# Graph attention with a pre-norm: the next group's norm, softmax and attention moved within the group, and a two-level product scheme for the second projection

## The chip, the cores and the metric

The kernel runs on one core of one Trainium2 chip. A core has five engines with their own instruction queues: TensorE multiplies matrices (the profile shows its weight loads apart, as PEld), VectorE (DVE), ScalarE (ACT) and GpSimd (POOL) work on tiles element by element, and SyncE (SP) issues transfers. The metric is the device time of one execution, in microseconds, and a kernel's time is the median of its runs.

## The reference

The input x has 128 graphs of 64 nodes with 512 features, in float32, and all graphs share one adjacency matrix of 64 x 64. Everything is computed in float32. Per graph:

```
h = relu(layernorm(x))
for each of 4 heads:  Wh = h @ W_head            # 512 x 512
    e = leaky_relu(f1[:, None] + f2[None, :])    # f = Wh . a, two scalars per node
    A = softmax(where(adj > 0, e, -1e9))         # 64 x 64
    head = elu(A @ Wh)
out = elu(one more such attention of concat(heads), with W_out: 2048 x 512)
y = relu(out @ w1 + b1) @ w2 + b2 + out
result = x + layernorm(y) * gamma + beta
```

## The kernel before

**Tiles and groups.** Rows of x are taken 128 at a time (two graphs make a tile), four tiles make a group (`G = 4`), and there are 16 groups. The loop over groups (`for g in range(NG)`, line 817) has two stages: a head stage, with the first projection of the four heads (`project1`), and a second stage with the second projection (`project2`). The other work is slipped between their steps.

**Products.** A 512 x 512 by 512 x 512 product is done on four quadrants of 256 with seven products in place of eight (Strassen's scheme in Winograd's form). `unit` (line 260) runs the seven products 1 to 7 in a given order and collects their sums in three PSUM banks, `after` moves sums out by VectorE and ScalarE, and `post` stores the results. One product has four float32 matmuls for each matrix, and each of those appears in the trace as two matmul instructions with 256 moving columns. The sums of weight quadrants are made once by `weight_sums` (line 199) on GpSimd and kept in device memory (`TC`); `piece` (line 227) loads one 256 KB piece of weights into a ring of 11 buffers, on SP's queue, ahead of its use. In `project2` the four heads are four matrices that add up in the same bank, so that it has 28 pieces; its operands are the four quadrant blocks `H1`, and GpSimd turns them in place into the sums that later products need (line 615).

**The group's attention.** Attention comes ahead of the head projection: A is applied to the normalized rows, and then the head's weights. `norm1` (line 352) normalizes one tile: statistics on VectorE, a power and a product on GpSimd, the activation on ScalarE. `transpose_h` and `project_f` give the scores, `attn_weights` runs the softmax on VectorE and ScalarE, `transpose_weights` turns the weights, `attend1` (line 510) multiplies, its results go through the six PSUM banks shared with the products (tag `mm`) and are copied half by ScalarE and half by VectorE. `z_sums` makes the operand sums of a head on GpSimd. `stage_a` (line 480) collects norm, scores and turns of a group.

**Around the second projection.** The list of steps of `project2(g)` is interleaved by `run` and `mix` with attention of group g+1 (`attend1`, then `z_sums` for its first head), norm and softmax of group g+2, and the feed-forward of group g-1 (`feed_forward`, line 690: transposes, two units of seven products, and `finish`, which normalizes a tile and stores it). The second attention of group g-1 (`stage_e`) stands in the head stage of g. In group 0 the head stage has norm and scores of group 1 and the weight sums of W_out.

**Order.** The order in which a helper is called gives priorities; a planner that works with estimated costs and with the buffers of each tag orders the instructions of every engine from these, and `tc.high_priority(AHEAD)` raises the evacuations. Each engine and SP's queue then work strictly in that order, so that an instruction that waits holds all behind it.

The lines that set the order of the second stage for an inner group are

```
run(project2(g), first + mix(
    ff[:7] + early + ff[7:12] + fin[:1] + ff[12:13] + fin[1:2] + ff[13:],
    scores + [nothing] * 8,
) + mix(fin[2:], [nothing] + turns + [nothing] * 2))
```

Of the kernel before, what the change touches and what calls it, by code (L numbers as in the profile page):

```python
# [18 lines left out]
AHEAD = 150  # L19


@with_exitstack
def gat_preln_kernel(
# [47 lines left out]
    ring = ctx.enter_context(tc.tile_pool(name="ring", bufs=11))  # L71
# [20 lines left out]
    def load(t, name="x"):  # L92

        tl = wk.tile([P, F], FP, tag="x", name=f"{name}{t}", bufs=4)
        nc.sync.dma_start(out=tl, in_=xf[ts(t, P), :])
        return tl
# [47 lines left out]
    MT, TC = {}, {}  # L144
    DIRECT = {}

    def fetch(m):
        MT[m] = big.tile([P, KC, O], FP, tag=homes[m], name=f"pw{m}")
        queue = nc.scalar if m < H else nc.gpsimd
        queue.dma_start(out=MT[m], in_=mats[m].rearrange("(k p) o -> p k o", p=P))  # L150
# [13 lines left out]
    def turn_a():  # L164

        rows = H * 2 * KC
        pt = aux([P, rows], "pah")
        nc.tensor.transpose(pt, ah, ident[0:rows, 0:rows])
        aT = wk.tile([P, H, 2, KC], FP, tag="s1", name="aT")
        nc.scalar.copy(aT.rearrange("p h c o -> p (h c o)"), pt)  # L170
        return aT

    def fold_dve(m, ab):

        for k in range(KC):
            for c in range(2):
                junk = wk.tile([P, O], FP, tag="t", name=f"jk{c}_{m}_{k}")
# [21 lines left out]
    def weight_sums(m, after=None):  # L199
# [20 lines left out]
        TC[m] = [dram.tile([P, 2, 2, Q], FP, name=f"tc{m}_{i}") for i in range(2)]  # L220
# [19 lines left out]


    late = []
# [17 lines left out]
    def unit(name, product, post, order):  # L260
# [5 lines left out]
        def after(p):  # L266
            if p in (1, 5, 6):
                nm = {1: "s1", 5: "s5", 6: "t"}[p]
                sb[nm] = wk.tile([P, 2, T], FP, tag=nm, name=f"{nm}_{name}")
# [30 lines left out]
    def product_t(m, blocks):  # L300

        def product(p):
            def fn(bk, start):
                w, a = piece(m, p), blocks(p)
                for o in range(2):
                    for k in range(2):
                        nc.tensor.matmul(  # L307
# [6 lines left out]
    def product_n(ms, blocks):  # L314

        def product(p):
            def part(i):
                def fn(bk, start):
                    w, a = piece(ms[i], p), blocks(p, i)
                    for k in range(2):  # L320
                        for j in range(2):
                            nc.tensor.matmul(  # L322
# [17 lines left out]
    def norm_stats(src, tag, t):  # L340

        st = sm.tile([P, 6], FP, tag=tag + "st", name=f"{tag}st{t}")
        nc.vector.bn_stats(st, src)
        mv = sm.tile([P, 2], FP, tag=tag + "mv", name=f"{tag}mv{t}")
        nc.vector.bn_aggr(mv, st)
        ve = sm.tile([P, 1], FP, tag=tag + "ve", name=f"{tag}ve{t}")
        nc.vector.tensor_scalar(ve, mv[:, 1:2], EPS, None, ALU.add)  # L347
        rstd = sm.tile([P, 1], FP, tag=tag + "rs", name=f"{tag}rs{t}")
        nc.gpsimd.tensor_tensor(rstd, ve, mhalf, ALU.pow)
        return mv[:, 0:1], rstd  # L350

    def norm1(t):
        if t not in X:
            X[t] = load(t)
        mean, rstd = norm_stats(X[t], "n1", t)
        nb = sm.tile([P, 1], FP, tag="n1nb", name=f"n1nb{t}")
        nc.gpsimd.tensor_scalar(nb, mean, rstd, -1.0, ALU.mult, ALU.mult)
        HN[t] = big.tile([P, F], FP, tag="hn", name=f"hn{t}", bufs=G)
        nc.scalar.activation(HN[t], X.pop(t), AF.Relu, bias=nb, scale=rstd)
        if t % G >= 2:  # L360
            HNS[t] = big.tile([P, T], FP, tag="hns", name=f"hns{t}", bufs=2)
            nc.gpsimd.tensor_tensor(HNS[t], HN[t][:, 0:T], HN[t][:, T:2 * T], ALU.add)
# [12 lines left out]
    def project_f(g):  # L375
# [15 lines left out]
        eng = nc.vector if g == 0 else nc.gpsimd  # L391
        eng.tensor_tensor(
# [65 lines left out]
    A1, E1, LAST = {}, {}, {}  # L458
# [4 lines left out]
    def transpose_weights(p):  # L463
        A = A1.pop(p)
        for j in range(2):
# [7 lines left out]
            AT[t] = big.tile([P, NB, H, N], FP, tag="at", name=f"at{t}", bufs=G)  # L473
# [6 lines left out]
    def stage_a(g):  # L480


        if g >= NG:
            return [], [], []
        p, r = 2 * g, 2 * g + 1

        def norms(p):
            norm1(2 * p)
            norm1(2 * p + 1)
            if p >= 2:  # L490
                prefetch(2 * p + 2)
                prefetch(2 * p + 3)

        def transposes(p):
# [3 lines left out]
        return (  # L498
            [lambda: norms(p), lambda: norms(r)],
            [  # L500
                lambda: transposes(p), lambda: transposes(r), nothing, lambda: project_f(g), nothing,
                lambda: (scores1(g), attn_weights(p)), nothing, lambda: attn_weights(r),
            ],
            [nothing, lambda: transpose_weights(p), nothing, nothing, lambda: transpose_weights(r)],
        )
# [4 lines left out]
    def attend1(g):  # L510
# [3 lines left out]
        def task(j, half):  # L514
# [6 lines left out]
            banks = [bank(f"pz{nm}_{t}_{b}") for b in range(NB)]  # L521
# [8 lines left out]
            for b in range(NB):  # L530
# [3 lines left out]
                if b == 0:  # L534
# [28 lines left out]
    def project1(g, h):  # L563
# [11 lines left out]
        def post(what, a, b=None, to=None):  # L575
# [8 lines left out]
            if what == "c21":  # L584
                nc.gpsimd.tensor_tensor(dst, dst, H1["22"][:, h], ALU.add)  # L585

# [15 lines left out]
    WH2 = {}  # L602

    def project2(g):
        slot = {1: "11", 2: "12", 3: "12", 4: "22", 5: "S1", 6: "11", 7: "S1"}
        h1 = dict(H1)
        wh = big.tile([P, G, FO], FP, tag="wh2", name=f"wh2_{g}")
        WH2[g] = wh

        def post(what, a, b=None, to=None):  # L610
            behind = {"s1": ("11", "S1", "11"), "s5": ("S1", "22", "11"), "c11": ("12", "12", "11")}
            if what in behind:
                dst, x0, x1 = (h1[n] for n in behind[what])
                for h in range(H):
                    nc.gpsimd.tensor_tensor(dst[:, h], x0[:, h], x1[:, h], ALU.subtract)  # L615
# [11 lines left out]
            f"b{g}", product_n(ms, lambda p, i: h1[slot[p]][:, i]), post, (1, 5, 6, 2, 7, 3, 4)  # L627
# [5 lines left out]
    def scores2(g, j):  # L633
# [3 lines left out]
        for c in range(2):  # L637
            junk = wk.tile([P, FO], FP, tag="elu", name=f"jf{g}_{j}_{c}", bufs=3)
            nc.vector.scalar_tensor_tensor(  # L639
                junk, WH2[g][:, j], 1.0, ao[:, c, :], ALU.mult, ALU.mult,  # L640
# [30 lines left out]
    def attend2(g, j):  # L671
        pa = aux([P, FO], f"pa2_{g}_{j}")
        nc.tensor.matmul(pa, AT2[g][:, j, :], WH2[g][:, j, :], start=True, stop=True)  # L673
# [16 lines left out]
    def feed_forward(g):  # L690
# [42 lines left out]
        def post2(what, a, b=None, to=None):  # L733
# [5 lines left out]
            eng = nc.vector if what[0] == "c" else nc.gpsimd  # L739
            eng.tensor_tensor(dst, a, dst, ALU.add)  # L740

        def finish(j):
            t = G * g + j
            xr = load(t, "xr")
            nc.gpsimd.tensor_tensor(xr, xr, bs, ALU.add)
            y = o[:, j]
            mean, rstd = norm_stats(y, "n2", t)
            nc.vector.scalar_tensor_tensor(y, y, mean, gs, ALU.subtract, ALU.mult)
            nc.vector.scalar_tensor_tensor(y, y, rstd, xr, ALU.mult, ALU.add)
            nc.sync.dma_start(out=of[ts(t, P), :], in_=y)  # L750

        f1 = unit(f"c{g}", product_t(M1, lambda p: bl[1][p]), post1, (1, 5, 6, 2, 3, 7, 4))
        f2 = unit(f"d{g}", product_n([M2], lambda p, i: bl[2][p]), post2, (1, 5, 6, 2, 3, 7, 4))
        return (
            [lambda j=j: transpose_out(j) for j in range(G)], f1 + f2,
            [lambda j=j: finish(j) for j in range(G)],
        )

    def mix(*lists):

        lists = [l for l in lists if l]
        keyed = [((i + 0.5) / len(l), n, fn) for n, l in enumerate(lists) for i, fn in enumerate(l)]
        return [fn for _, _, fn in sorted(keyed, key=lambda k: k[:2])]
# [4 lines left out]
    for t in range(G):  # L768
        norm1(t)
# [47 lines left out]
    for g in range(NG):  # L817
        if g >= 1:
            side = stage_e(g - 1)
        else:  # L820
            side = sum(stage_a(1), [])
            for i, m in ((5, 4), (9, 5), (12, 6), (17, 7)):
                side.insert(i, lambda m=m: more_sums(m))
# [10 lines left out]
        attn = attend1(g + 1) if g + 1 < NG else []  # L834
        norms, scores, turns = stage_a(g + 2)
        tr, ff, fin = feed_forward(g - 1) if g >= 1 else ([], [], [])
        if g == NG - 1:
            run(project2(g), tr + [nothing] * 6 + ff[:2])
# [56 lines left out]
```

## Time and profile before

| | us |
|---|---|
| median of 3 runs | 2363.31 (2363.18 to 2363.83) |
| the profiled execution | 2362.2 |
| its span, first to last instruction | 2360.4 |
| matmul busy (TensorE) | 2317.9, 98% |
| weight loads busy | 1934.5, 82% |
| VectorE busy | 1265.5, 54% |
| GpSimd busy | 1026.7, 43% |
| ScalarE busy | 911.0, 39% |
| moved by transfers | 366.89 MB, 155 GB/s in the mean |
| mean granted TensorE clock | 0.992 |

The products dominate the chain that ended last: 33% of the span are matmuls of the second projection (g_b), 32% of the first (g_a), and 8% each of the two feed-forward units (g_c, g_d). A busy matmul row is not the time that TensorE needs for it, since matmuls overlap: their spacing is read from the start times in the timeline. Names in rows are the kernel's tiles with buffer numbers left out, moving and stationary operand after the arrow, and a line can be that of a helper.

### The profile page before, as it was taken

What the parts mean: (1) busy time and instruction counts of PE and PEld (TensorE: products, weight loads), DVE (VectorE), ACT (ScalarE), POOL (GpSimd) and SP (SyncE); (2) the same over time, 40 slices, a digit from 0 to 9 for tenths busy, and PEclk for the clock granted to TensorE, in tenths of its full rate; (3) what the DMA queues carried; (4) which work ended last, traced back from release to release, by engine and by line L of the source; (5) the groups of instructions that cost most, each with busy time, mean ns of one, the idle gap of its engine ahead of it and who ended that gap; (6) DMA issues with size and microseconds to landing.
All of it is one profiled execution on the core that took longest, in us unless ns stands there. A gap on an engine that the chain in (4) does not pass through costs nothing.

```text
span 2360.4 us, 32849 instructions
## 1 busy us (share of the span) xinstructions
PE 2317.9 (98%) x11805; PEld 1934.5 (82%) x11805; DVE 1265.5 (54%) x2210; ACT 911.0 (39%) x1623; POOL 1026.7 (43%) x917
## 2 busy tenths in 40 slices
PE   6989999999999999999999999999999999999997
PEld 4868787888878888787887878888788887878885
DVE  7625474554646556474554745556464563744527
ACT  2524425253352533425244251533525344251513
POOL 5664444416344353443524444253443534533333
PEclk7999999999999999999999999999999999999999
DMA  8545353444535445353444544435354453534443
GB/s 308 184 142 193 125 183 127 164 152 132 182 125 178 134 139 179 126 180 129 154 163 129 182 131 161 153 130 181 127 177 132 138 179 127 182 118 164 157 148 106
DMA packets 257809, 366.89 MB, mean 155 GB/s; under 512 B 22216, under 2 KB 145128, under 8 KB 257648
## 3 DMA queue, kind: packets, MB, share of 16 engines
q1 hardware_dynamic: 251024, 343.82, 43.9%
q0 software_dynamic: 4512, 16.78, 1.9%
q10 hardware_dynamic: 2112, 4.19, 0.5%
q8 instruction: 95, 1.56, 0.3%
q14 instruction: 66, 0.54, 0.1%
HBM read 337.45 MB, written 27.26 MB: 155 GB/s over the span
## 4 chain that ended last, share of the span: by engine, by line
PE 94%; DVE 2%; ACT 1%; POOL 1%; issue 0%; DMA 0%; DVEq 0%
PE g_b L322 33%; PE g_a L307 32%; PE g_c L307 8%; PE g_d L322 8%; PE pz L525 4%; PE pa L673 2%; PE pto L700 1%; PE pzS L525 1%; PE pth L371 1%; PE s1pt L472 1%; PE pf L381 1%; PE s1pe L406 1%; DMA x<-in_x_dram 0%; PE s2pt L667 0%; PE pwa L193 0%
## 5 line engine op out<-in xcount | busy, mean ns | idle before, releaser
L322 PE MATMUL g_b<-w,h 128*128 128x256 f32 x2560 | 598.1, 381 | 0.0
L322 PEld LDWEIGHTS g_b<-w,h 128*128 128x128 f32 x2560 | 480.5, 190 | 72.2 <-issue 10.1
L307 PE MATMUL g_a<-z,w 128*128 128x256 f32 x1520 | 361.0, 380 | 1.2 <-DVE g_a L581 0.7
L307 PE MATMUL g_a<-zs_z,w 128*128 128x256 f32 x1504 | 347.9, 379 | 0.0
L307 PEld LDWEIGHTS g_a<-z,w 128*128 128x128 f32 x1520 | 287.6, 190 | 57.9 <-issue 14.3
L307 PEld LDWEIGHTS g_a<-zs_z,w 128*128 128x128 f32 x1504 | 284.8, 190 | 50.5 <-issue 14.3
L322 PE MATMUL g_b<-w,hS 128*128 128x256 f32 x1024 | 243.5, 382 | 0.0
L585 POOL TENSOR_TENSOR hS<-hS,h 128x512 f32<-128x512 f32 x64 | 83.0, 1297 | 366.8 <-DVE hS L549 366.8
L547 ACT ACTIVATE exc<-g_a 128x512 f32<-128x512 f32 x256 | 152.3, 595 | 199.7 <-DVE g_a L581 119.6
L322 PEld LDWEIGHTS g_b<-w,hS 128*128 128x128 f32 x1024 | 191.4, 191 | 30.9 <-issue 6.7
L549 DVE SCALAR_TENSOR_TENSOR h<-exc,g_a 128x512 f32<-128x512 f32 x192 | 131.6, 686 | 136.3 <-ACT exc L548 136.2
L548 ACT ACTIVATE exc<-exc 128x512 f32<-128x512 f32 x256 | 161.6, 631 | 6.5
L615 POOL TENSOR_TENSOR h<-h,h 128x512 f32<-128x512 f32 x64 | 86.7, 1362 | 138.1 <-PE g_b L322 138.0
L332 POOL TENSOR_TENSOR zs_z<-zS,z 128x512 f32<-128x512 f32 x63 | 89.7, 1424 | 128.3 <-PE g_a L307 123.7
L615 POOL TENSOR_TENSOR h<-hS,h 128x512 f32<-128x512 f32 x64 | 81.1, 1268 | 142.4 <-PE g_b L322 142.4
L474 ACT COPY at<-s1pt 128x512 f32<-128x512 f32 x64 | 34.7, 588 | 279.8 <-PE s1pt L472 279.8
L307 PE MATMUL g_c<-ot,w 128*128 128x256 f32 x512 | 123.9, 385 | 0.8 <-DVE n2ve L347 0.8
L322 PE MATMUL g_d<-w,rt 128*128 128x256 f32 x512 | 121.5, 380 | 1.7 <-DVE o L740 1.0
L307 PE MATMUL g_a<-zS,w 128*128 128x256 f32 x496 | 117.2, 379 | 0.0
L639 DVE SCALAR_TENSOR_TENSOR jf<-wh,ao 128x512 f32<-128x512 f32 x128 | 94.3, 776 | 40.3 <-ACT wh L621 40.1
L333 POOL TENSOR_TENSOR zs_z<-z,zs_z 128x512 f32<-128x512 f32 x63 | 85.4, 1357 | 61.1 <-PE g_a L307 40.7
L307 PEld LDWEIGHTS g_c<-ot,w 128*128 128x128 f32 x512 | 93.9, 190 | 21.8 <-issue 9.3
(159 smaller groups left out, 3535.6 us busy)
## 6 DMA issues: line engine op xcount, KB each, us to landing
w<-tc SPq DMA_DIRECT2D x632, 256.0 KB, 2.6
w<-in_L_gnn_W_heads_dram SPq DMA_DIRECT2D x192, 256.0 KB, 2.7
w<-in_L_gnn_W_out_dram SPq DMA_DIRECT2D x192, 256.0 KB, 2.7
w<-in_L_gnn_w_dram SPq DMA_DIRECT2D x96, 256.0 KB, 2.7
x<-in_x_dram SPq DMA_DIRECT2D x66, 256.0 KB, 3.6
xr<-in_x_dram SPq DMA_DIRECT2D x64, 256.0 KB, 2.8
out_dram<-o SPq DMA_DIRECT2D x64, 256.0 KB, 2.1
tc<-pt POOLq DMA_DIRECT2D x20, 512.0 KB, 5.6
```

The lines of the kernel that those rows point to most:

```text
L307: nc.tensor.matmul(bk[:, o, :], w[:, k, ts(o, P)], a[:, k, :], start=start and o == 0 and k == 0, stop=k == 1, skip_group_check=True,)
L322: nc.tensor.matmul(bk[:, j, :], a[:, k, ts(j, P)], w[:, k, :], start=start and k == 0 and j == 0, stop=i == len(ms) - 1 and k == 1, skip_g ...
L332: eng.tensor_tensor(s2, s1, a11, ALU.subtract)
L333: eng.tensor_tensor(s4, a12, s2, ALU.subtract)
L525: nc.tensor.matmul(banks[b][:, c, :].rearrange("p (h n) -> p h n", h=H), src[rows, off + c * P:off + (c + 1) * P], at[rows, b], start=True ...
L547: nc.scalar.activation(ex, src, AF.Relu, scale=-1.0)
L548: nc.scalar.activation(ex, ex, AF.Exp, scale=-1.0)
L549: nc.vector.scalar_tensor_tensor(dst, ex, -1.0, src, ALU.add, ALU.max)
L585: nc.gpsimd.tensor_tensor(dst, dst, H1["22"][:, h], ALU.add)
L615: nc.gpsimd.tensor_tensor(dst[:, h], x0[:, h], x1[:, h], ALU.subtract)
L639: nc.vector.scalar_tensor_tensor(junk, WH2[g][:, j], 1.0, ao[:, c, :], ALU.mult, ALU.mult, accum_out=f[:, c, j:j + 1],)
L673: nc.tensor.matmul(pa, AT2[g][:, j, :], WH2[g][:, j, :], start=True, stop=True)
```

## The change

Three things change together.

**The order of a group's attention.** Norm, softmax and attention of group g+1 all come within group g. `norms1(g+1)` stands in the head stage (entry 15 of its side list), with its first instruction made to wait for the latest matmul before it (`behind_pe`); the tiles of x are loaded straight into the buffers in which they are normalized, and the loads for group g+2 follow each attention task. `attention_tasks` gives scores, softmax and turns places between 0.02 and 0.50 of the second stage, `attend1` follows from 0.55 to 0.90, `z_sums` at 0.93, and the feed-forward has places of its own. All are merged by these places with the steps of the second projection. Attention's results go through the two auxiliary PSUM banks and are copied by ScalarE alone after group 0; turned weights share the buffers of turned activations.

**The second projection of groups 3 to 15** (`DEEP = 3`) uses two levels of the seven-product scheme. Each of the seven outer products of 256 is done by seven products of 128, so 49 parts, each with a piece of 128 x 128 weights for all four heads (256 KB) and one float32 matmul of 128 columns per head. `quarter_sum` makes the operand sums, in one buffer for each kind; `inner` combines the seven results of each quadrant; sums within H1 are made in the head stage. The weight sums for it are made by `block_sums` in the head stages of groups 1 to 3, and read back from device memory. Results lie in a buffer with seven slots for each quadrant.

**Smaller parts.** The reciprocal square root of the norms is done for four or two tiles at once by a bit pattern and three Newton steps on VectorE, in place of GpSimd's power; R of the scores and two additions of the feed-forward move from GpSimd to VectorE; `finish` takes two tiles at a time; the weights' ring has 12 buffers; feed-forward units beside a two-level projection run their products in the order 1, 2, 5, 6, 3, 7, 4.

The diff, cut to its core:

```diff
-    ring = ctx.enter_context(tc.tile_pool(name="ring", bufs=11))
+    ring = ctx.enter_context(tc.tile_pool(name="ring", bufs=12))
...
+        if name == "x":
+            tl = big.tile([P, F], FP, tag="hn", name=f"hn{t}", bufs=G)
...
+    def block_sums(p, i):
+        heads = slice(2 * i, 2 * i + 2)
+        y = big.tile([P, 2, 2, 2, P], FP, tag=f"ot{i}", name=f"y{p}_{i}")
+        for h in range(2):
+            nc.gpsimd.dma_start(
+                out=y[:, h].rearrange("p k c o -> p k (c o)"),
+                in_=out_block(p, slice(2 * i + h, 2 * i + h + 1))[:, 0],
+            )
+        t = big.tile([P, 4, 2, P], FP, tag=f"rt{i}", name=f"ty{p}_{i}")
...
+        nc.gpsimd.dma_start(out=TQ[p][:, :, heads], in_=t)
+
+    def small_piece(p, j):
+        w = ring.tile([P, H, P], FP, tag="w", name=f"wq{p}_{j}")
...
+        nc.sync.dma_start(out=w, in_=src)
+        return w
...
+            nc.vector.tensor_tensor(u, y, y, ALU.mult)
+            nc.vector.tensor_tensor(u, u, hv, ALU.mult)
+            nc.vector.scalar_tensor_tensor(y, u, 1.5, y, ALU.add, ALU.mult)
...
-            banks = [bank(f"pz{nm}_{t}_{b}") for b in range(NB)]
+            banks = [aux([P, 2, T], f"pz{nm}_{t}_{b}") for b in range(NB)]
...
-                if b == 0:
+                if b == 0 or g > 0:
                     nc.scalar.copy(dst, srcv)
...
+            if g >= DEEP and h >= H - 2:
+                heads = slice(0, H - 1) if h == H - 2 else slice(H - 1, H)
+                for n in {"c11": ["11"], "c12": ["12"], "c21": ["S1", "22"]}.get(what, []):
+                    q = H1[n][:, heads, :, P:]
+                    nc.gpsimd.tensor_tensor(q[:, :, 0], q[:, :, 0], q[:, :, 1], ALU.add)
...
+    def project2_deep(g):
+        outer = (1, 2, 5, 6, 3, 7, 4)
...
+        def quarter_sum(p, j):
+            x = h1[SLOT[p]]
+            eng = nc.gpsimd if p in (3, 7, 4) else nc.vector
+            q = QS[p, j] = wk.tile([P, H, P], FP, tag=f"q{j}", name=f"q{j}_{p}_{g}", bufs=1)
...
+                w, x = small_piece(p, j), operand(p, j)
+                for h in range(H):
+                    LAST["pe"] = nc.tensor.matmul(
+                        bk[:, place[j][1]], x[:, h], w[:, h], start=first and h == 0,
+                        stop=h == H - 1, skip_group_check=True,
+                    )
...
+        tasks += [(0.01 + 0.03 * i, fn) for i, fn in enumerate(tr)]
+        tasks += [(0.16 + 0.05 * i, fn) for i, fn in enumerate(ff[:7])]
+        tasks += [(0.54 + 0.058 * i, fn) for i, fn in enumerate(ff[7:])]
+        tasks += [(0.84, fin[0]), (0.97, fin[1])]
+        steps = second(g)
+        tasks += [((i + 0.5) / len(steps), fn) for i, fn in enumerate(steps)]
+        for _, fn in sorted(tasks, key=lambda k: k[0]):
+            fn()
```

## The prediction

> **What bounds the kernel now.** I read the page's busy shares first, then the chain that ended last, the timeline of TensorE inside one group, and the table of windows. Shares, and the chain in order of time around one group (start us, us, what):
>
> ```profile
> PE 2317.9 (98%) x11805; PEld 1934.5 (82%) x11805; DVE 1265.5 (54%) x2210; ACT 911.0 (39%) x1623; POOL 1026.7 (43%) x917
> ...
> 1191.45 15.54 PE g_a L307 x72
> ...
> 1334.41 15.54 PE g_a L307 x72
> ```
>
> TensorE is the bound, and the head stage begins again every 1334.41 - 1191.45 = 142.96 us. Windows of one group, head stage then second projection (us; busy us and count of PE, PEld, DVE, ACT, POOL; clock; DMA share; GB/s):
>
> ```profile
> 1048.50:1105.00 56.50, 56.50 (x262) 47.42 (x263) 30.72 (x57) 32.20 (x57) 13.55 (x11) 1.00 0.44 146
> 1105.00:1191.50 86.50, 86.50 (x477) 72.32 (x474) 47.43 (x77) 24.55 (x46) 46.99 (x43) 1.00 0.47 155
> ```
>
> No other engine passes 57% in either. So only shorter TensorE issue shortens a group. Timeline of TensorE (start, us, line, operation, moving and stationary, shape, count):
>
> ```profile
> 1128.37 1.04 PE L371 MATMUL pth<-ident,hn 128*128 128x128 f32 x8
> 1129.25 1.89 PE L307 MATMUL g_c<-ot,w 128*128 128x256 f32 x8
> 1130.97 1.89 PE L322 MATMUL g_b<-w,h 128*128 128x256 f32 x8
> ...
> 1140.58 1.08 PE L381 MATMUL pf<-hT,wa 128*32 128x128 f32 x32
> 1141.59 2.00 PE L307 MATMUL g_c<-zs_o,w 128*128 128x256 f32 x8
> ```
>
> From start to start: eight 256-column instructions take 1130.97 - 1129.25 = 1.72 us, 215.75 ns each by neighbouring rows; eight 128-column transposes take 0.88 us, 109-110 ns each, every one behind a weight load of its own.
>
> **The skill.** The Trainium skill, "TensorE: Matmul & The Clock Gate", section "LDWEIGHTS (loading the stationary operand)", prices a weight load by its columns: 128/1.2 = 107 ns. The trace agrees: the group pwa, 128-column loads with matmuls of only two columns, took 6.84 us for 32 at half clock (window 28.6 to 35.4: clock 0.50), 214 ns, so 107 at full clock. "Back-to-back issue gap" there says that in a stream of pairs "the per-MM spacing is set by *both* ops", with 81 ns sustained at N=128 against 56 alone. The transposes don't show this, but their loads are shorter (141 ns recorded against 190), so they don't settle it. "SBUF — State Buffer", section "Who interferes with whom", says that a VectorE operation with two SBUF inputs and a GpSimd read exclude each other; L710 shows it, 693 ns alone and up to 1831.
>
> **The change, part by part.**
>
> Second projection of groups 3 to 15 (13 groups). Removed: 7 products x 4 heads x 4 matmuls x 2 passes = 224 instructions (3584/16 in the page's g_b rows) x 215.75 = 48.33 us. Added: 7 x 7 x 4 x 2 = 392 of 128 columns. Lower bound 109 ns (the transposes; also pf, whose four 32-column strips each repeat every 109 ns). Upper for a hidden load: 107 plus the few ns by which loads beside a matmul are longer than lone ones (190 against 186), plus start, 115. I take 110: 43.12 us, a gain of 5.21 a group, 13 x 5.21 = 67.7. At 109: 5.60 and 72.8; at 115: 3.25 and 42. Even is 48.33/392 = 123.3 ns.
>
> Weights. 49 pieces of 256 KB instead of 28 on SP's queue. A piece lasts TensorE 8 x 0.110 = 0.88 us; SP issues one in 0.33-0.38. Engine time: 1 KB packets take 46 ns at the median, 2 KB 84; 512-byte ones I estimate at 27 (between the 18 of 256 bytes and 46). So 21 pieces of 512-byte rows x 32 x 27 = 18.1 us, 28 x 8 x 84 = 18.8, other loads and stores of the stage (some 26 x 0.7) 18: 55 of about 82 us. At 46 ns for the small ones it is 68, still under. Twelve ring slots cover 10 us; landing was 2.6-2.7. Cost 0; without the cover up to 1 us per late piece.
>
> Sums of operands. 21 additions of 128x512: twelve on VectorE (0.69, 1.8 when excluded: 8 to 21 us), nine on GpSimd (1.35: 12). Inner sums: five operations, 1792 elements, on each engine (2.6 to 6; 4.7). Evacuations: more and smaller, +2 us on VectorE, +2 on ScalarE. Pre-sums of H1 in the head stage: four times 512 elements, 5.4 us of GpSimd. Moved: eight z copies from VectorE to ScalarE (8 x 0.687 off, 8 x 0.585 on), R to VectorE (+1), two additions of L740 to VectorE (+1.4), the powers of L349 off GpSimd (8, 6 us), 13 tiny operations of about 0.15 us per norm call on VectorE (three calls, 6 us, for 8 removed). VectorE in the second projection then: 47.4 - 5.5 - 3.9 (norm gone to the head stage) + 1 + 1.4 + 8..21 + 3..6 + 2 + 3 = 56 to 72 of 82 us; GpSimd 47 + 17 - 12 = 52; ScalarE about 30. None becomes the bound by its sum.
>
> Order. The norm's gate puts bn_stats on VectorE behind a matmul; behind it queue the ELUs of the head stage, which have three spare PSUM banks, a head's 14 us. Softmax at 0.20 and 0.26, weights turned at 0.42 and 0.50 of about 82 us: two chains of ten operations, some 15 us of work, in 18 and 20 us. Attention at 0.55 to 0.90 in the two auxiliary banks: two copies of 0.585 each 4 us. z sums from 0.93: GpSimd needs 1.4 us for the first, wanted by the third product, 3.5 us into the head. x loads for the next group but one wait on SP for the attention that frees their tile; the loads are used half a group later. PSUM: a two-level product holds up to four of the six banks that matmuls share (two halves each of two sums), the feed-forward unit two; a late evacuation of either delays the other's next product. Turned weights take the four buffers that turned activations had, which project_f frees at 0.13. Each is covered in the mean, with a few us to spare; I take 0.75 us a group exposed, +10 (0 to 4 a group).
>
> Products of W_out for two levels (groups 1 to 3): 14 units of four additions (1.32) and three GpSimd issues (0.58), 7 us each, 33 us per head stage beside 20.6 that GpSimd has there, of 56. Nearly full: z sums and hS additions queue behind. +3 (0 to 8).
>
> Start. Group 0 loses TensorE time to x tiles fetched late:
>
> ```profile
> 129.31 5.66 DMA x<-in_x_dram
> 135.00 0.69 DVE n1st L343
> 135.69 0.60 DVE z L537
> 136.34 2.07 PE pzS L525 x6
> ...
> 143.56 2.61 DMA x<-in_x_dram
> ```
>
> This work is no longer in group 0's second projection: about 5.7 + 2.3 = 8 us off (+5 to -12, since group 1's softmax now has no group of lead).
>
> End. Inner sums (2.7) ahead of the last softmax, and a norm of two tiles with the chain of small operations after the last matmul: +3 (1 to 6).
>
> Sum against the profiled execution's own 2362.2 (span 2360.4 and 1.8 around it): 2362.2 - 67.7 + 10 + 3 - 8 + 3 = 2302.5. The median of the runs is 1.1 higher: 2304.
>
> **Rivals.**
> 1. Forecast, 0.62: TensorE stays the bound at 109-112 ns: 2304, own range 2284 to 2325.
> 2. Stalls take part of it, 0.20: the quarter sums have one buffer each, so the next outer product's sum waits for the last read and must be ready seven pieces (6 us) later; a queue holding two excluded additions (3.6) or the four behind-sums (5.4) uses that up. For it: VectorE up to 72 of 82 us. Against: the kernel before has no such gap after 190 us. At 2.5 to 3 us a group: 2304 + 13 x 2 to 2.3 = 2330 to 2335.
> 3. The weight load shows, 0.08, slower: spacing by both operations. With the skill's ratio 81/56 on 109 ns, 158 ns: 392 x 0.158 = 61.9, +13.6 a group, 2304 + 67.7 + 13 x 13.6 = 2548. It ends slower than before as soon as a pass exceeds about 122 ns (there the 8 us of the other terms, 0.6 a group, are no longer paid for). Against: pwa and the transposes overlap fully.
> 4. Attention doesn't fit into one group, 0.06, slower: softmax or z sums late at each of 15 starts; it decides from 60/15 = 4 us. At 6 us: 2304 + 90 = 2394.
> 5. Both about even, 0.04: 2363.
>
> **How the numbers follow.** Below 0.2% (4.7 us), about what a measurement of this kernel can tell from no change, I call it the same. Faster: 1, 2 and a little: 0.83; same 0.04; slower 3 and 4: 0.13. Range 2282 to 2348: it takes in 109 ns with no stall (2304 - 5 - 10 - 4 = 2285, less some) and 3.5 us of stall a group or 115 ns with some (2304 + 26 + 13 = 2343); outside lie cases 3 to 5 and a tail.
>
> **What would show it.** Right: head stages from group 3 on begin every 138 us; the new matmuls start 109-112 ns apart; no gap before pieces. Wrong: spacing over 120 ns with loads that start only when the matmul before ends; TensorE waiting for a quarter sum, for at, for aux banks, or for w with the ring empty; SP waiting for pz; the first 190 us longer.

## The result and the profile after

The changed kernel takes 2531.06 us (median of 3 runs, 2528.75 to 2531.25) against 2363.31: the ratio is 1.0706, 95% interval 1.0682 to 1.0731. The profiled execution took 2528.75, its span is 2526.4, and the mean granted TensorE clock fell from 0.992 to 0.967. The prediction said 2304.

Busy shares from the page of the changed kernel, and the shares of its chain by engine:

```profile
PE 2323.4 (92%) x13989; PEld 2001.3 (79%) x13989; DVE 1631.8 (65%) x2909; ACT 995.9 (39%) x1808; POOL 1296.1 (51%) x1062
...
PE 61%; DVE 12%; issue 8%; POOL 8%; ACT 5%; DMA 4%; SPq 1%; DVEq 0%; POOLq 0%; ACTq 0%
```

TensorE was 94% of the chain and is now 61%. VectorE, GpSimd and unexplained issue have taken most of the rest. Windows of one steady group, first the head stage (from the group's first g_a to its first g_b) and then the second stage, with the columns of the prediction's table:

```profile
1117.33:1181.12 63.79, 54.83 (x236) 45.67 (x235) 45.15 (x101) 31.55 (x55) 27.54 (x23) 0.92 0.44 137
1181.12:1269.83 88.71, 87.60 (x671) 78.87 (x669) 57.07 (x82) 31.17 (x60) 50.55 (x38) 1.00 0.70 208
```

Cut in the same way, a group of the kernel before:

```profile
1048.33:1099.25 50.92, 50.92 (x231) 43.38 (x230) 27.36 (x52) 28.33 (x51) 11.69 (x9) 1.00 0.45 149
1099.25:1191.29 92.04, 92.04 (x506) 76.35 (x505) 50.78 (x82) 28.41 (x51) 48.84 (x44) 1.00 0.46 153
```

The second stage, where the two-level products are, became 3.3 us shorter. The head stage, whose products didn't change, became 12.9 us longer, at a clock of 0.92. TensorE's timeline shows where, in the head stage that begins at 661.8:

```profile
668.68 1.89 PE L365 MATMUL g_a<-zs_z,w 128*128 128x256 f32 x8
679.37 3.75 PE L365 MATMUL g_a<-zs_z,w 128*128 128x256 f32 x8 [8.80 <-issue]
682.92 2.19 PE L365 MATMUL g_a<-z,w 128*128 128x256 f32 x8
684.94 1.89 PE L365 MATMUL g_a<-zS,w 128*128 128x256 f32 x8
```

Ahead of product 7 of the group's first head TensorE stands for 8.80 us, and then the first eight matmuls take 3.75 us in place of 1.89. This gap comes back in every head stage from group 4 on. (Below, gaps are counted from the start of the last matmul ahead of them, as in the expectations; this one is 9.2 in that count.) The bracket says only "issue". The list of waits leads further: its largest row, with total, times and longest wait, is the copy (by ScalarE) that saves what product 6 left in a bank, before product 7 adds to the same bank.

```profile
ACT t_a L331 <- DVE g_a L330: 247.4, 61, 16.2
```

The copy waits for `after`'s addition for product 6 (L330) on VectorE. In the gap above the copy runs from 678.69 to 679.27, and TensorE starts at 679.37. (The page's chain leads back over a load of xr and GpSimd's z sums instead. The last of these operations ends at 670.61, 8.8 us before TensorE starts, so they don't end the wait.) VectorE's timeline shows what it did ahead of that addition:

```profile
656.89 1.74 DVE L816 SCALAR_TENSOR_TENSOR jf<-wh,ao 128x512 f32<-128x512 f32 x1 [3.60 <-POOL wh L752]
...
663.59 0.68 DVE L919 TENSOR_TENSOR o<-g_d,o 128x512 f32<-128x512 f32 x1
664.30 1.29 DVE L414 BATCH_NORM_STATS2 n2st<-o 128x6 f32<-128x512 f32 x2
...
666.49 1.23 DVE L421 TENSOR_SCALAR n2v<-n2mv 128x2 f32<-128x2 f32 x1
667.64 1.84 DVE L929 SCALAR_TENSOR_TENSOR o<-o,n2mv,gs 128x512 f32<-128x512 f32 x1
...
674.03 0.69 DVE L746 TENSOR_TENSOR wh<-wh 128x512 f32<-128x512 f32 x1
...
676.73 0.69 DVE L816 SCALAR_TENSOR_TENSOR jf<-wh,ao 128x512 f32<-128x512 f32 x1
...
677.96 0.69 DVE L330 TENSOR_TENSOR g_a<-g_a,s_a 128x512 f32<-128x512 f32 x1
```

The queue is one unbroken line from 656.89. First, the score of the first tile (jf, for the second attention of the group that is ending) waits 3.60 us for GpSimd to end `inner(0)` (L752). It and three more scores take 1.74 us each instead of 0.69, beside GpSimd's z sums. Then come the norm of the last two tiles, 9.8 us with its small operations, the five operations of `inner(1)`, and two more scores. L330 comes 16.2 us after the head stage began. In the kernel before it comes 5.5 us after (at 624.90, the stage begins at 619.4), and there VectorE waits for TensorE:

```profile
624.90 0.70 DVE L272 TENSOR_TENSOR g_a<-g_a,s_a 128x512 f32<-128x512 f32 x1 [1.21 <-PE g_a L307]
```

Wherever a steady head stage of these runs has the gap, TensorE starts again 1.4 us after L330, whether L330 comes 8.0 us (inner_out below), 11.7 (fin_gated), 12.2 (late4), 14.2 (pow) or 16.2 us after the stage began; where it comes within 6.8 us there is no gap. Product 7 is due 8.6 us into the stage (five products of 1.73), so the addition may come some 7.2 us into it at no cost (an estimate: 8.6 less 1.4).

### The profile page after: what moved, and what is told of

Same layout as the page of the kernel before. It is cut to its first block, busy times and chain, and to the rows that moved or that the text cites. A ratio compares the mean times of both kernels' runs of the same rounds, so it can differ in the third digit from the quotient of the medians.

```text
span 2526.4 us, 38939 instructions
## 1 busy us (share of the span) xinstructions
PE 2323.4 (92%) x13989; PEld 2001.3 (79%) x13989; DVE 1631.8 (65%) x2909; ACT 995.9 (39%) x1808; POOL 1296.1 (51%) x1062
## 4 chain that ended last, share of the span: by engine, by line
PE 61%; DVE 12%; issue 8%; POOL 8%; ACT 5%; DMA 4%; SPq 1%; DVEq 0%; POOLq 0%; ACTq 0%
PE g_a L365 18%; PE g_b L762 17%; PE g_c L365 7%; PE g_d L380 6%; PE pz L594 3%; PE g_b L380 3%; DMA xr<-in_x_dram 2%; POOL xr L925 2%; POOL zs_z L392 1%; POOL zs_z L390 1%; PE pzS L594 1%; DVE n1st L414 1%; PE pth L454 1%; PE s1pt L554 1%; ACT hn L440 1%
## 5 line engine op out<-in xcount | busy, mean ns | idle before, releaser
L762 PE MATMUL g_b<-wq,q 128*128 128x128 f32 x2184 | 286.2, 276 | 4.2 <-POOL q L708 2.1
L762 PEld LDWEIGHTS g_b<-wq,q 128*128 128x128 f32 x2184 | 267.8, 192 | 15.9 <-issue 8.0
L762 PE MATMUL g_b<-wq,h 128*128 128x128 f32 x2080 | 272.3, 277 | 0.0
L762 PEld LDWEIGHTS g_b<-wq,h 128*128 128x128 f32 x2080 | 254.0, 192 | 17.5 <-issue 13.0
L604 ACT COPY z<-pz 128x512 f32<-128x512 f32 x186 | 100.1, 588 | 245.4 <-PE pz L594 245.4
L816 DVE SCALAR_TENSOR_TENSOR jf<-wh,ao 128x512 f32<-128x512 f32 x128 | 143.5, 1165 | 48.1 <-POOL wh L752 47.5
L925 POOL TENSOR_TENSOR xr<-xr,bs 128x512 f32<-128x512 f32 x64 | 87.4, 1374 | 131.7 <-DMA xr<-in_x_dram 110.4
L686 POOL TENSOR_TENSOR hS<-h,h 128x512 f32<-128x512 f32 x64 | 87.3, 1390 | 77.3 <-PE g_b L762 60.8
L882 POOL TENSOR_TENSOR o<-o,b2s 128x512 f32<-128x512 f32 x64 | 92.8, 1467 | 56.7 <-PE pto L880 50.5
L594 PE MATMUL pz<-at,hn 64*128 64x256 f32 x768 | 118.3, 413 | 0.0
```

Of the source, the lines that this page charges most:

```text
L594: nc.tensor.matmul(banks[b][:, c, :].rearrange("p (h n) -> p h n", h=H), src[rows, off + c * P:off + (c + 1) * P], at[rows, b], start=True ...
L604: nc.scalar.copy(dst, srcv)
L762: LAST["pe"] = nc.tensor.matmul(bk[:, place[j][1]], x[:, h], w[:, h], start=first and h == 0, stop=h == H - 1, skip_group_check=True,)
L816: nc.vector.scalar_tensor_tensor(junk.rearrange("p (c v o) -> p c v o", c=2, v=2), WH2[g][j], 1.0, ao[:, c, :].rearrange("p (c v o) -> p c ...
L882: nc.gpsimd.tensor_tensor(o[:, j], o[:, j], b2s, ALU.add)
L925: nc.gpsimd.tensor_tensor(x_, x_, bs, ALU.add)
```

## The experiments

Each run has the kernel before timed beside it. Differences below are against that (2364.6 to 2366.8), or differences of such differences; the diffs are against the changed kernel. The expectations name their theories by letters. In order_alone, fin_gated, nogate, combo3, gate_all and order_gate, D is that VectorE's queue at the start of a head stage binds; A says this in inner_out, pow and late4, and in order_pow and pow D is a rival.

### Which part costs what

These kernels take the parts out one after another.

**order_alone** leaves out the two-level scheme and the block sums, and keeps the new order, norm and placement.

```diff
-DEEP = 3
+DEEP = 16
```

> The two-level scheme is left out for all groups (DEEP = 16, so no block sums either); the new order of norm, softmax and attention stays. Theory D (VectorE's queue at the start of a head stage: the addition of product 6 of head 0 stands behind six score products and the norm of two finished tiles, and TensorE stops at product 7 until it and the copy behind it are done): the same queue, short of the inner sums (2.7 us) and of the wait for GpSimd's inner sums (3.6), so a stall of 2 to 6 us stays at each head stage, 2400 to 2470 us. Rival P (the two-level products themselves, their weight loads or their pieces): the stall goes with them, 2355 to 2385.

Measured: 2403.19, ratio 1.0155 (1.0138 to 1.0172). The new order alone loses 36.8 us: theory D's range for the time holds, but the gap in each head stage is 1.2 us, not 2 to 6. Head stages come every 144.3 us (before: 143.0). Head stage 1 starts at 197.2 (190.6), the last period is 144.3 (137.0), and from the last head stage to the end it takes 181.3 (174.3).

**blocks_only** adds to this the block sums in the head stages of groups 1 to 3, whose results nothing reads.

```diff
-            if g >= DEEP and h >= H - 2:
+            if False and h >= H - 2:
...
-        second = project2_deep if g >= DEEP else project2
+        second = project2
```

> The two-level products are left out, but the sums of W_out's blocks for them are still made and stored in the head stages of groups 1 to 3. Theory B: these sums hold GpSimd's queue while they wait for their loads, and z sums behind them come late; order_alone (2403) plus the 25 to 40 us that groups 1 to 3 lost: 2425 to 2445, with the gaps near 205 and 368 us. Rival: those gaps belong to VectorE's queue as in the later groups: 2400 to 2410.

Measured: 2439.53, ratio 1.0326 (1.0304 to 1.0348), 74.9 over before, in theory B's range. The block sums cost 38 us. The periods from head stages 1, 2 and 3 are 158.3, 156.6 and 150.3; from group 4 on they are 144.3 again. GpSimd's timeline at the first of them:

```profile
206.79 0.71 POOL L280 TENSOR_TENSOR ty<-y 128x256 f32<-128x256 f32 x1 [2.37 <-DMA y<-in_L_gnn_W_out_dram]
...
212.06 0.71 POOL L280 TENSOR_TENSOR ty<-y 128x256 f32<-128x256 f32 x1 [0.72 <-DMA y<-in_L_gnn_W_out_dram]
...
215.23 0.73 POOL L284 DMA_DIRECT2D tq<-ty  x1 [0.30 <-POOL ty L283]
215.93 2.55 POOL L390 TENSOR_TENSOR zs_z<-zS,z 128x512 f32<-128x512 f32 x2
```

And TensorE's timeline of the same kernel there:

```profile
202.95 1.89 PE L365 MATMUL g_a<-zS,w 128*128 128x256 f32 x8
217.32 2.93 PE L365 MATMUL g_a<-zs_z,w 128*128 128x256 f32 x6 [12.48 <-POOL zs_z L390]
```

The z sums that the head's third product needs stand in GpSimd's queue behind block sums, and these stand waiting for their own loads. By these lines it isn't a matter of 33 + 20.6 us fitting into 56, but of who stands ahead of the z sums; no run put the z sums first.

**sums_out** is the changed kernel without any of the two-level sums. Products, loads and block sums stay.

```diff
-            if g >= DEEP and h >= H - 2:
-                ...
-                return QS[p, j]
-            c, r = {1: (0, 0), 2: (1, 0), 5: (0, 1), 4: (1, 1)}[j]
+            c, r = {3: (0, 1), 6: (0, 0), 7: (1, 0), 1: (0, 0), 2: (1, 0), 5: (0, 1), 4: (1, 1)}[j]
...
-                        if p == 7:
-                            inner(0, nc.gpsimd)
-                        if p == 4:
-                            inner(1, nc.vector)
-                if j in (6, 7, 3) and p != outer[-1]:
-                    quarter_sum(outer[outer.index(p) + 1], j)
```

> The changed kernel with the two-level sums left out: no quarter sums, no sums of halves before the second projection, no inner sums behind it. All deep products, their loads and the block sums of groups 1 to 3 stay. The output lacks those sums. Theory A (the sums, on VectorE and GpSimd, cost the steady groups their time, and the deep products are as fast as their spacing says): a steady period is that of the new order alone, 144.3 us, less the 4.4 us that the products save, so 139 to 142 us, no gap of over 3 us in a steady head stage, and the whole about 2403 + 36 for the block sums - 13 x 4.4 = 2382 (2365 to 2400). Theory B (the deep products themselves, by their many loads, small pieces and shorter accumulations, slow TensorE or its clock): periods stay over 148 us and the whole over 2480.

Measured: 2381.66, ratio 1.0073 (1.0056 to 1.0089), a steady period of 140.2, one gap of 1.0 to 1.1 us in each steady head stage and none longer. Theory A holds: with the evacuations that go with them the deep products save 58.4 us against blocks_only, 4.5 a group, and the sums around them cost what the changed kernel takes more than this one.

**inner_out** leaves out the ten inner sums alone.

```diff
-                        if p == 7:
-                            inner(0, nc.gpsimd)
-                        if p == 4:
-                            inner(1, nc.vector)
```

> The changed kernel with the ten inner sums (five on GpSimd, five on VectorE) behind the second projection left out; quarter sums and sums of halves stay. The output lacks the inner sums. Theory A (VectorE's queue at the seam is what binds, and the inner sums put 3.6 us of waiting for GpSimd, 2.7 us of work and a later start of the head's z sums into it): the gap of 9.2 us falls to 0 to 3 us, the clock behind it stays up, periods 141 to 145 us, the whole 2531 - 12 x (7 to 10) = 2410 to 2447. Theory C (the quarter sums and the norm's chain are as much to blame as the inner sums): the gap stays over 5 us and the whole over 2470.

Measured: 2401.75, ratio 1.0158 (1.0143 to 1.0174). The period is 141.4, the gap is 1.0 us. Theory A holds, and the effect is 8 us beyond its range. Ten operations, some 5 us of work on GpSimd and 2.7 on VectorE in a group, are worth 131 us. Windows of one steady group of inner_out, head stage and second stage:

```profile
1088.16:1140.92 52.76, 51.87 (x236) 43.56 (x235) 37.70 (x85) 31.34 (x55) 22.93 (x20) 1.00 0.52 165
1140.92:1229.60 88.68, 87.59 (x670) 78.86 (x669) 61.30 (x94) 31.23 (x60) 49.01 (x35) 1.00 0.69 209
```

The second stage is as long as with the inner sums (88.71); the head stage is 11.0 us shorter, and at full clock. VectorE's timeline shows why:

```profile
640.48 0.69 DVE L812 SCALAR_TENSOR_TENSOR jf<-wh,ao 128x512 f32<-128x512 f32 x1
...
654.84 0.68 DVE L738 TENSOR_TENSOR wh<-g_b,wh 128x512 f32<-128x512 f32 x1
658.48 0.69 DVE L915 TENSOR_TENSOR o<-g_d,o 128x512 f32<-128x512 f32 x1 [2.96 <-PE g_d L380]
...
672.04 0.69 DVE L330 TENSOR_TENSOR g_a<-g_a,s_a 128x512 f32<-128x512 f32 x1
```

(This kernel is four lines shorter: L812 here is L816 there, L915 is L919.) Without `inner(0)` the first four scores are free to run at 640.48, in the second stage; and after L738 VectorE idles for the last g_d instead of waiting for GpSimd. L330 comes 8.0 us after the head stage began, about as in order_alone (8.2).

**order_pow** and **pow** take the Newton chain back to one power on GpSimd, in order_alone and in the changed kernel.

```diff
-        nc.vector.tensor_scalar(hv, v, -0.5, None, ALU.mult)
-        ...
-        for _ in range(3):
-            nc.vector.tensor_tensor(u, y, y, ALU.mult)
-            nc.vector.tensor_tensor(u, u, hv, ALU.mult)
-            nc.vector.scalar_tensor_tensor(y, u, 1.5, y, ALU.add, ALU.mult)
+        nc.gpsimd.tensor_tensor(y, v, mhalf.to_broadcast([P, n]), ALU.pow)
```

> The new order alone, without the two-level scheme, with the norm's Newton chain replaced by one power on GpSimd. Theory A (the 1.2 us gap of each head stage, and part of the late start, come from the chain on VectorE ahead of product 7's operations): the gap goes, periods 143 us, the whole 2403 - 13 x 1.2 = 2387 (2380 to 2395). Rival D (the power waits in GpSimd's queue as long as the chain takes): 2400 to 2415.

Measured: 2386.83, ratio 1.0091 (1.0076 to 1.0106); most periods are 143.2, and the end after the last head stage fell from 181.3 to 175.4. Theory A's direction holds: the chain costs 15 us of order_alone's loss. That the forecast of 2387 is met to the microsecond is luck. It was 13 gaps of 1.2 us, but by the profiled runs the periods from head stage 1 on give 11 us, the end 5.9, and head stage 1 starts 4.3 later (201.5, against 197.2); three head stages still have gaps of 0.6 to 1.6. Of the 21.7 us that are left over the kernel before, 10.9 lie ahead of head stage 1 and 6.2 in the last period (143.2, against 137.0). What makes the start late no run settles.

> The changed kernel with the norm's Newton chain of 12 small VectorE operations replaced by one power on GpSimd, as the kernel before had it. Theory A (everything ahead of product 6's addition in VectorE's queue counts): the two chains of a group lie ahead of it in the second stage and at the seam, of which the seam's one spans some 5 us; but the power waits in GpSimd's queue behind z sums or inner sums, so part comes back: the gap falls from 9.2 to 3 to 8 us, the whole 2440 to 2515. Rival D (the chain's operations fill time in which VectorE would wait for GpSimd anyway): same within 10 us, 2520 to 2540.

Measured: 2504.33, ratio 1.0586 (1.0568 to 1.0604). The gap falls to 7.2 us, the period to 149.8: theory A at the weak end of its range. In VectorE's timeline of pow the chain is replaced by a wait of 0.60 us, and `inner(1)` and two scores still follow:

```profile
678.61 2.41 DVE L922 SCALAR_TENSOR_TENSOR o<-o,n2y,xr 128x512 f32<-128x512 f32 x2 [0.60 <-POOL n2y L421]
```

The parts add up, taken out in this order: new order without the chain +21.7, chain +15.1, block sums +38.1, deep products -58.4, quarter sums and sums of halves +20.1, inner sums +131.1. The sum, before rounding, is the 167.8 us of the result, each term a difference of excesses over the kernel before. (It adds up by construction; what the runs give is the size of each term, and another order of removal would share them out a little differently.)

### Moving the queue about

Five more kernels keep everything and move what stands ahead of product 6's addition; a sixth makes such moves in order_alone.

**late4** puts four empty places ahead of the scores in the head stage's list instead of one, so they come three places later.

```diff
-            gap + score + [lambda: spread2(g)] + gap * 2 + [lambda: softmax2(g)] + gap * 5
+            gap * 4 + score + [lambda: spread2(g)] + gap * 2 + [lambda: softmax2(g)] + gap * 5
```

> The changed kernel with the scores of the second projection four places later in the head stage, nothing left out. VectorE's order at the seam is then: norm of the last two tiles, inner sums, product 6's addition, and only then the eight scores; the 3.6 us of waiting for GpSimd's inner sums and six of the scores (some 8.4 us) are no longer ahead of the addition. Theory A (it is the wait of the scores for the inner sums, not the inner sums' own time, that makes the queue late): VectorE still finds the last product of the feed-forward part only 5 us later, so the addition moves forward by 3 to 6 us, the gap falls from 9.2 to 3 to 6 us, the period from 152 to 146 to 149 us, the whole to 2455 to 2495, if softmax and attention do not come late for it. Rival (the inner sums' own time and what GpSimd does beside them binds): the gap stays over 7 us, the whole over 2510.

Measured: 2490.91, ratio 1.053 (1.0509 to 1.0551); the gap is 5.2 us, the period 147.3, both as theory A has it. L330 comes 12.2 us after the head stage began. From VectorE's timeline ahead of it, before `inner(1)`:

```profile
685.12 1.19 DVE L428 TENSOR_TENSOR n2u<-n2u,n2h 128x2 f32<-128x2 f32 x1
686.35 1.19 DVE L429 SCALAR_TENSOR_TENSOR n2y<-n2u,n2y 128x2 f32<-128x2 f32 x1
687.57 0.16 DVE L427 TENSOR_TENSOR n2u<-n2y 128x2 f32<-128x2 f32 x1
```

With the scores gone some small operations of the norm fall beside GpSimd's z sums, and take 1.19 us in place of 0.16. So part of what the move frees is lost to the next in line. The start lost too: head stage 4 begins at 680.5 (661.8 in the changed kernel). Of this 7.5 us lie ahead of head stage 1; in head stages 2 and 3 there are stalls of 5.5 and 2.8 us for the late scores, and in 3 another of 4.1 for one of VectorE's additions.

**fin_gated** moves the norm of the last two tiles into the next head stage, behind product 7 of its first head, with a wait for the latest matmul.

```diff
-            tasks += [(0.84, fin[0]), (0.97, fin[1])]
+            tasks += [(0.84, fin[0])]
+            carry = lambda f=fin_raw[g - 1]: f(2, True)
...
+            if carry is not None:
+                side.insert(6, carry)
```

> Two-level scheme kept; only the norm of the last two tiles of the group before is moved, behind product 7 of head 0. Theory D: some 9.8 us of VectorE's work no longer stand ahead of product 6's addition; the gap of 9.2 us in each head stage falls to 0 to 3 and TensorE's clock no longer drops behind it: 12 x 8 to 11 us less, 2400 to 2440. Rival P: unchanged, 2520 to 2535. Rival S (SP's queue held by the stores, so that head weights come late): gap shrinks only if the stores move too, with TensorE waiting for w in the trace.

Measured: 2476.61, ratio 1.0468 (1.0451 to 1.0485), the best of these, but 37 us above theory D's range. The gap falls to 4.7 us, not to 0 to 3, and L330 to 11.7 us after the start. The norm's 9.8 us gave back only half: `inner(1)` then runs beside the z sums, and its five operations take 7.0 us instead of 2.7.

**nogate** takes the wait for TensorE off the inner sums.

```diff
-            behind_pe(eng.tensor_tensor(
+            eng.tensor_tensor(
                 m[:, :, 1:6:4], m[:, :, 1:6:4], m[:, :, 0:1].to_broadcast(two), ALU.add
-            ))
+            )
```

> Only the wait of the inner sums for the latest matmul is taken out, so that GpSimd's five can start after product 3. Theory D: VectorE's idle 3.6 us for GpSimd's wh ahead of the scores go, and part of their lengthening by GpSimd (4 x 1.05): gap 9.2 to 2..6, 2450 to 2495. Rival P: unchanged.

Measured: 2555.4, ratio 1.0787 (1.0753 to 1.082), slower than the changed kernel, where theory D had 2450 to 2495. The wait for `inner(0)` moved into the second stage, ahead of the feed-forward's evacuations, and TensorE's gap with it:

```profile
662.65 3.78 PE L380 MATMUL g_d<-w,rt 128*128 128x256 f32 x8 [7.42 <-DVE o L919]
...
683.43 2.07 PE L365 MATMUL g_a<-zs_z,w 128*128 128x256 f32 x5 [2.45 <-issue]
```

**combo3** is fin_gated and nogate together, with three empty places ahead of the scores instead of one.

> Moved norm, no wait of the inner sums, and the scores of the second attention three places later. Theory D: no gap in head stages from group 4 on, periods of 139 to 141 us; what is left over the kernel before is the start and groups 1 and 2 (some 39 us): 2365 to 2400. Rival P: periods stay at 150 or more.

Measured: 2558.28, ratio 1.0813 (1.0781 to 1.0845), a miss by over 150 us. The gap in the head stage is gone, but TensorE stands 6.5 us in the second stage and 3.3 ahead of turning the second attention's weights; the period is 153.5.

**gate_all** puts the scores, `inner(1)` and the norm's end all behind product 7 of the first head.

```diff
-                            inner(1, nc.vector)
+                            INNER[g] = lambda: inner(1, nc.vector)
...
+            if j == 0 and c == 0 and g < NG - 1:
+                behind_pe(first)
...
-            gap + score + [lambda: spread2(g)] + gap * 2 + [lambda: softmax2(g)] + gap * 5
+            gap * 8 + [lambda: INNER.pop(g, lambda: None)()] + score + [lambda: spread2(g)] + gap * 2 + [lambda: softmax2(g)] + gap * 4
```

> Two-level scheme kept. All that stood on VectorE ahead of product 6's addition in a head stage is made to wait for product 7 of head 0 and put behind it: VectorE's inner sums, the scores of the second attention, the norm of the last two tiles. Theory D (VectorE's queue, lengthened by waits for GpSimd and by exclusion): the gap of 9.2 us and the slower clock behind it go, periods from group 4 on 139 to 142 us, 2380 to 2420 us. If the gap stays in the same place with VectorE's addition done early, it is another wait (weights, z sums), and the time stays above 2470.

Measured: 2482.45, ratio 1.049 (1.0464 to 1.0517), 62 us above theory D's range. VectorE reaches L330 in time, after 10.29 us of idling. Then a product of head 1 waits 3.6 us while VectorE works on the moved norm and scores, and there are some 1 to 2 us of waiting in three more places; the period is 147.3.

**order_gate** is these moves and waits in order_alone.

> The new order alone (two-level scheme left out), with the same waits as gate_all. Theory D: the 1.2 us gaps of order_alone in each head stage go, 14 x 1.2: 2380 to 2392. If order_alone's loss is elsewhere (start, end): 2398 to 2408.

Measured: 2494.11, ratio 1.0549 (1.0534 to 1.0565): a miss. The period rose from 144.3 to 150.8. The moves and waits cost 6.5 us a group by themselves where there is little to gain.

No version beats the kernel before. sums_out, with all sums gone, still takes 16.6 us more than it does, so that the order's start and end and the block sums would have to be mended first. fin_gated or late4 together with pow wasn't tried.

## Why the prediction was wrong, point by point

**The step that failed** is the pair "Sums of operands" and "Order". The first added up engine time for the second stage and closed with "None becomes the bound by its sum". As loads its figures were right: VectorE's second stage was forecast at 56 to 72 us and is 57.07, GpSimd's at 52 and is 50.55. The head stage, where the time was lost, got no such sum for VectorE, whose work there went from 27.36 to 45.15 us; that is still less than the stage took before (50.92). But the bound was not a sum. It was one addition, product 6's, in VectorE's queue at the seam between two stages, which came 16.2 us into the head stage where some 7.2 would have cost nothing. "Order" listed what queues behind the norm's gate and took 0.75 us a group. It looked at the new norm in the head stage, and not at the seam, where the scores and inner sums of a group and the end of the feed-forward's norm of the one before meet the first products of the next. The inner sums were priced as 2.6 to 6 us of an engine, and as time of the kernel only in the term "End" (2.7). That the scores read their results, and so have to wait for them at the seam, was in the code and was missed. Measured: 131 us where the sum had nothing for the steady groups but the general 0.75 a group.

**The products** were sized well. Forecast 110 ns and 67.7 us; the median spacing of the new matmuls is 112 ns (before: 216), or 4.5 us a group, and taking blocks_only and sums_out together they save 58.4. In the timeline of the changed kernel:

```profile
736.61 1.16 PE L762 MATMUL g_b<-wq,h 128*128 128x128 f32 x8
737.60 1.06 PE L762 MATMUL g_b<-wq,q 128*128 128x128 f32 x8
```

**The transfers** cost nothing, as forecast. Ahead of g_b<-wq,q TensorE is idle for 4.2 us in all over 2184 matmuls, and its weight loads wait 1.3 us for wq.

**Block sums**, "+3 (0 to 8)": 38. The work was even counted too high: an addition has 256 columns and takes 0.71 us, not 1.32, so that a head stage has some 23 us of it in place of 33 (an estimate: 14/3 units of four additions and three issues of 0.73). The queues were named, but the waits of a block sum for its own load stand in that queue too.

**Tiny operations**, "6 us" of VectorE's time a group and none of the kernel's: 15.1 us of order_alone's time, by order_pow. One takes 0.16 us (forecast: about 0.15), or 1.2 beside GpSimd's z sums.

**Start**, "-8 (+5 to -12)": head stage 1 begins 12.2 us later than before (202.8 against 190.6), 6.6 of it in order_alone already. **End**, "+3 (1 to 6)": 19.5 more from the last head stage on (193.8 against 174.3), of which order_alone has 7.0 and, without the chain, order_pow 1.1.

**The rivals.** 2 had the right kind of effect in the wrong place: quarter sums and sums of halves cost 1.2 us a group (141.4 against 140.2). 3 comes nearest in time (2548), by luck, since its mechanism isn't there: the loads don't show at 112 ns. Of 4 there is 0.9 us a group, in which TensorE waits for R of the softmax (L474; 1.23 us from start to start, 0.31 in the kernel before); for turned weights and attention it doesn't wait in a steady group. Half of this is counted in the 1.2 of rival 2, since without the sums it is 0.4. That the next stage's evacuation could stand behind this stage's rest was in none of them.

**What the clock adds.** The Trainium skill, "TensorE: Matmul & The Clock Gate", section "Part 1: The HAM clock gate (the "warmup" mystery)", says that TensorE falls to half its rate after an idle window of some 3.4 us and comes back after one that is busy. The traces agree for the long gaps: after 8.80 us idle, and after 4.79 in late4, the first eight matmuls take 3.75 us; after 0.64 in inner_out they take 1.97. On the length they differ: in nogate matmuls are at half rate after 2.45 us already (five take 2.07 in the row shown with nogate), so the idle time that it takes can be shorter than the page says. From the restart to the third set of eight it takes 5.57 us (679.37 to 684.94), and 3.53 in inner_out. So of the 10.6 us by which the period is longer than in inner_out (152.0 against 141.4) 8.2 are the gap (start of eight to start of eight, 10.69 against 2.54) and 2.0 the clock.

## What to carry to other kernels

An engine with a third of its time free can still set the end, if its queue is in order and an evacuation on which the next product hangs stands behind work that could wait. For every moved or added operation ask two things: which instruction of the next stage stands behind it, and which other engine's result it waits for there. Small operations on VectorE and GpSimd are priced by what the other runs beside them (a score took 0.69 or 1.74 us, five inner sums 2.7 or 7.0), so a move that frees one place can lengthen what takes it.

## What the runs showed of the hardware

The Trainium skill, "SBUF — State Buffer", section "SBUF: two separate sides", says that a VectorE instruction with two SBUF inputs and a GpSimd instruction that reads SBUF exclude each other, and that whoever comes second blocks for the whole instruction. The 1.74 us of a score and the 1.19 us of a two-element operation beside GpSimd's z sums (0.69 and 0.16 alone) agree: each takes 1.03 to 1.05 us longer, most of one GpSimd operation (1.27). I had not expected that this can last over several. In VectorE's timeline of blocks_only:

```profile
361.11 0.16 DVE L428 TENSOR_TENSOR n2u<-n2u,n2h 128x2 f32<-128x2 f32 x1
361.30 6.82 DVE L429 SCALAR_TENSOR_TENSOR n2y<-n2u,n2y 128x2 f32<-128x2 f32 x1
```

And in GpSimd's timeline of the same kernel:

```profile
361.85 2.56 POOL L390 TENSOR_TENSOR zs_z<-zS,z 128x512 f32<-128x512 f32 x2
364.31 2.54 POOL L391 TENSOR_TENSOR zs_z<-z,zs_z 128x512 f32<-128x512 f32 x2
366.75 1.31 POOL L925 TENSOR_TENSOR xr<-xr,bs 128x512 f32<-128x512 f32 x1
```

The operation of two elements ends when a train of five back-to-back GpSimd operations ends, at 368.1. It is no accident of one run: in the changed kernel one such operation of the same chain takes 6.74 us (at 362.2), and in inner_out, nogate and late4 one takes 6.73 to 6.81. Why a hold sometimes lasts one operation and sometimes five, no run here settles.
